# Softmax denominators spread to the heads' rows through DRAM instead of through TensorE

## The chip, the cores and the metric

The kernel runs on one core of one Trainium2 chip. The metric is the time of one execution on the device in microseconds (us), median of several runs. All numbers in this document are of this kernel: run times, one profiled execution, and the answers of its trace. A core has five engines that each follow their own instruction queue in order: TensorE (PE in the profile, with its weight loads as PEld), VectorE (DVE), ScalarE (ACT), GpSimd (POOL) and SyncE (SP). [...] Transfers are issued by SP, ACT or POOL and run on the core's 16 DMA engines.

## The reference

The input x is (2, 256, 64, 64), float32. Layer 0 is attention over all 4096 pixels of an image, with 8 heads of 32 channels, and a 1x1 convolution behind it:

```python
q = proj(Wq, bq) / math.sqrt(hd)
k = proj(Wk, bk)
v = proj(Wv, bv)
attn = jax.nn.softmax(jnp.einsum('bnd,bmd->bnm', q, k), axis=-1)
fuse = jnp.einsum('bnm,bmd->bnd', attn, v)
fuse = fuse.transpose(0, 2, 1).reshape(B, C, H, W)
hybrid = _conv1x1(jnp.concatenate([x, fuse], axis=1), Wf, bf)
return hybrid * m + x * (1.0 - m)
```

Layer 1 is a channel gate, attention in windows of 8x8 pixels with 4 heads, two grouped 7x7 convolutions with normalisation, and a sigmoid gate:

```python
x = x * jax.nn.sigmoid(a.transpose(0, 3, 1, 2))
...
attn = jax.nn.softmax(jnp.einsum('whqd,whkd->whqk', q, k) * hd ** (-0.5), axis=-1)
...
y = lax.conv_general_dilated(x, sa_w1, (1, 1), [(3, 3), (3, 3)], dimension_numbers=dn, feature_group_count=cr)
...
y = lax.conv_general_dilated(y, sa_w2, (1, 1), [(3, 3), (3, 3)], dimension_numbers=dn, feature_group_count=cr)
...
return x * jax.nn.sigmoid(y)
```

What the change touches is the division in layer 0's softmax: fuse is the sum of exp(score) times v, divided by the sum of exp(score), one such sum for each head and each query pixel.

## The kernel before

The program has three parts in time. First (to about 186 us) q, k and v of both images are computed and stored in DRAM. Then comes a long pipeline over 1024 slots (to about 2754 us), and then a tail that finishes the convolutions (to the end at 2980 us).

A slot is one (image b, chunk c of 512 query pixels, head group g of four heads, block m of 128 keys): 2 x 8 x 2 x 32. In a slot, `scores` lets TensorE compute the scores of four heads (L633) two slots ahead, ScalarE takes their exp (L646, three instructions) into a tile e, `products` multiplies them with v into the accumulator av (L665), and VectorE adds e to a running total of 128 keys x 4 heads x 512 pixels (L667). There are eight buffers for e, so VectorE may be up to eight slots late before an exp has to wait for it. A chunk is 64 slots: its two head groups, one after the other.

After a chunk's last slot its work is handed to a small planner. `at(delay, action)` puts an action into a list, due so many slots later, and `run_later` performs the due ones at the end of each slot. DN is 8. The list for a chunk is: `denominators` (DN: 64 pairs of weight load and matmul records on TensorE, L688, which sum the totals over keys; a ScalarE copy to the tile inv, L695), the reciprocal of inv on VectorE (DN+1, L721), the spread of the reciprocals to the rows of their heads in two halves (DN+2 and DN+4, TensorE L704 and ScalarE L711, into the tile rd), the multiplication f = f * rd on VectorE (DN+5, L724), and `stage` (appended at DN+6). inv holds one reciprocal per head and pixel: at partitions 32q to 32q+7, heads 0 to 7 for the q-th quarter of the chunk's pixels. rd holds the same values repeated over the 32 channels of each head: 128 partitions x 2 x 512. For the very first chunk the steps after the reciprocal are `late` by nine slots, the stage by thirteen.

`stage` is a generator that carries a chunk through the 1x1 convolution and the window attention. `run_stages` gives it one step on every fourth slot. Its first step is L739: eight pairs of matmuls, four with x and then four with f, so that the second half needs L724. Then come L747 (ScalarE), L751 and L753 (VectorE). Its last step puts the chunk's result into xo (L971) and POOL stores it in DRAM (L986).

Each engine runs these instructions in the order in which the program makes them, since the section is scheduled by hand. An instruction that waits therefore holds up all that stands behind it on its engine.

The last chunk's actions run after the slots, in a loop that performs nothing but them and single steps of the convolution `conv` (L1052, L1076). There the last stage's steps and the convolution's alternate. The convolution's results go out by L1111 from POOL and SP.

Of the kernel before, what the change touches and what calls it, by code (L numbers as in the profile page):

```python
# [10 lines left out]
F32 = mybir.dt.float32  # L11
# [20 lines left out]
DN = 8  # L32
# [11 lines left out]
HALVES = (slice(0, 64), slice(64, 128))  # L44
# [12 lines left out]
def conv_seq_kernel(ctx: ExitStack, tc: tile.TileContext, a, out):  # L57
    nc = tc.nc
    const = ctx.enter_context(tc.tile_pool(name="const", bufs=1))
    dram = ctx.enter_context(tc.tile_pool(name="dram", bufs=1, space=bass.MemoryType.DRAM))  # L60
# [11 lines left out]
    def psum2(name):  # L72
        return ps["pair"].tile([P, 2, CH], F32, tag="s", name=name)
# [7 lines left out]
    ident = const.tile([P, P], F32, name="ident")  # L81
# [12 lines left out]
    nc.gpsimd.memset(keysum, 0.0)  # L94
    for h in range(HEADS0):
        nc.gpsimd.memset(keysum[:, h, :, h : h + 1], 1.0)
    spread_h = const.tile([P, KC, HG, HD0], F32, name="spread_h")

    for q in range(4):
        nc.gpsimd.tensor_copy(  # L100
            spread_h[32 * q : 32 * q + 32],
            ident[32 * q : 32 * q + 32, 32 * q : 32 * q + HEADS0]
            .rearrange("p (g j) -> p g j", g=KC)
            .unsqueeze(3)
            .to_broadcast([32, KC, HG, HD0]),
        )


    xo = const.tile([P, KC, WS, WP], F32, name="xo")
    nc.gpsimd.memset(xo, 0.0)  # L110
    cbias1 = const.tile([P, NU], F32, name="cbias1")
# [5 lines left out]
        for c in range(NCHUNK)  # L117
    }

    mask_s = dram.tile([B, NCHUNK, CH], F32, name="masks")  # L120


# [250 lines left out]
    with (  # L373
# [8 lines left out]
        for n in ("WqT", "WkT", "WvT"):  # L382
            t = w0.tile([P, KC, C], F32, name=n)
# [4 lines left out]
        for n in ("bq", "bk"):  # L388

            t = w0.tile([P, KC], F32, name=n)  # L390
# [31 lines left out]
        for i, (b, c) in enumerate(chunks):  # L422
# [43 lines left out]
        for i, (b, c) in enumerate(chunks):  # L466
            s = psum2(f"v0_{b}_{c}")
            sv = s.rearrange("p a (t o) -> p (a t) o", t=2)
            for m in range(4):
                for kc in range(KC):  # L470
# [4 lines left out]
                        start=(kc == 0),  # L475
                        stop=(kc == KC - 1),
# [21 lines left out]
            elif i == 2:  # L498
# [3 lines left out]
                for oc in range(KC):  # L502
                    for kc in range(KC):
# [4 lines left out]
                            start=(kc == 0),  # L508
                            stop=(kc == KC - 1),
# [13 lines left out]
    def pipeline(arm, shifted, pools):  # L523
# [23 lines left out]
        stages = deque()  # L547

        def at(delay, action):
            later.append((now[0] + delay, action))  # L550

        def load_piece(n):
            if n * PB >= len(slots):
                return
            b, c, g, m = slots[n * PB]
            p = m // PB
            nm_ = f"{arm}_{b}_{c}_{g}_{p}"
            k = kvp.tile([P, PB * P], F32, tag="k", name=f"k{nm_}")
# [95 lines left out]
        def products(i):  # L654
            b, c, g, m = slots[i]
            if m == 0:
                acc[0] = avp.tile([P, CH], F32, tag="av", name=f"av{arm}_{i}")
                acc[1] = ep.tile([P, HG, CH], F32, tag="sum", name=f"sum{arm}_{i}", bufs=3)
                totals[b, c, g] = acc[1]
            av, total = acc[0], acc[1]  # L660
            e, v = es[i], vts[b, c, g, m // PB]
            start, stop = m == 0, m == NMB - 1
            for j in range(HG):
                r = slice(32 * j, 32 * j + 32)
                nc.tensor.matmul(av[r, :], v[:, m % PB, r], e[:, j, :], start=start, stop=stop)  # L665
            if m > 0:
                nc.vector.tensor_add(total, first[0] if m == 1 else total, e)  # L667
            e = es.pop(i)
            if start:
                first[0] = e  # L670
            if stop:
                if g == 0:
                    fts[b, c] = fp.tile([P, KC, CH], F32, tag="f", name=f"f{arm}_{b}_{c}")
                f = fts[b, c]
                nc.scalar.copy(f[:, g, :], av)  # L675
                if g == 0:
                    return
                both = [totals.pop((b, c, gg)) for gg in range(KC)]
                inv = fp.tile([P, P], F32, tag="inv", name=f"inv{arm}_{i}")
                rd = fp.tile([P, KC, 4, P], F32, tag="rd", name=f"rd{arm}_{i}")  # L680


                def denominators():
                    s = psum2(f"dn{arm}_{i}")
                    for h in range(HEADS0):
                        for q in range(4):
                            r = slice(32 * q, 32 * q + 32)
                            nc.tensor.matmul(  # L688
                                s[r, 0, 0:P],
                                keysum[:, h].rearrange("p i h -> p (i h)"),  # L690
                                both[h // HG][:, h % HG, q * P : (q + 1) * P],
                                start=(h == 0),
                                stop=(h == HEADS0 - 1),
                            )
                    nc.scalar.copy(inv, s[:, 0, 0:P])  # L695


                def spread(hh):
                    t = psum2(f"rd{arm}_{i}_{hh}")
                    for gg in range(KC):  # L700
                        for q in range(2):
                            r = slice(64 * hh + 32 * q, 64 * hh + 32 * q + 32)
                            for o in HALVES:
                                nc.tensor.matmul(  # L704
                                    t[o, q, gg * P : gg * P + P],
                                    spread_h[r, gg].rearrange("p j d -> p (j d)")[:, o],
                                    inv[r, :],
                                    start=True,
                                    stop=True,
                                )  # L710
                    nc.scalar.copy(  # L711
                        rd[:, :, 2 * hh : 2 * hh + 2, :],
                        t[:, :, 0 : KC * P].rearrange("p q (g n) -> p g q n", g=KC),
                    )

                late = EB + 1 if (b, c) == (0, 0) else 0
                at(DN, denominators)  # L720
                at(DN + 1, lambda: nc.vector.reciprocal(inv, inv))  # L721
                at(DN + 2 + late, lambda: spread(0))
                at(DN + 4 + late, lambda: spread(1))
                at(DN + 5 + late, lambda: nc.vector.tensor_mul(f, f, rd.rearrange("p g q n -> p g (q n)")))  # L724

# [427 lines left out]
        def run_later():  # L1153
            for _ in range(len(later)):
                due, action = later.popleft()
                if due <= now[0]:
                    action()
                else:
                    later.append((due, action))
# [17 lines left out]
        for i, (b, c, g, m) in enumerate(slots):  # L1177
            now[0] = i
            if (b, c, g, m) == (B - 1, NCHUNK - 1, 0, 0):
                for _ in banded:  # L1180
                    pass
                conv = convolve()
                next(conv)
            if m % PB == 0:
                load_piece(i // PB + AHEAD)
            if g == KC - 1 and m == 0:
                nxt = (b, c + 1) if c + 1 < NCHUNK else (b + 1, 0)
                if nxt[0] < B:
                    load_q(*nxt)
            rest = scores(i + 2) if i + 2 < len(slots) else None  # L1190
            products(i)
            if rest:
                rest()
            if g == KC - 1 and m == NMB - 1:
                late = EB + 5 if (b, c) == (0, 0) else 0
                at(DN + 6 + late, lambda b=b, c=c: stages.append(stage(b, c)))
            run_later()
            if i % 5 == 1:
                next(banded, None)
            if i % 4 == 0:  # L1200
                run_stages()
# [102 lines left out]
```

## Time and profile before

| What | us |
|---|---|
| Median of 3 runs | 2982.66 (2981.29 to 2983.53) |
| The profiled execution | 2982.11, its span 2980.3 |
| L633 on TensorE (scores), busy | 1167.4 |
| L665 on TensorE (products), busy | 1091.9 |
| L667 on VectorE (adds), busy | 2198.8 and 73.0 (first adds) |
| L646 on ScalarE (exp), busy | 2038.4 |
| Rest of POOL before L986, waiting for L971 | 2523.8 |
| Granted TensorE clock, mean | 0.996 of full speed |

How to read it: the profile is of one execution, so its span is compared with its own time, 2982.11, and that with the median. "Busy" is the time in which an engine has an instruction in work. Matmuls overlap one another, so the sum of their durations is far above their busy time, and a TensorE that is always busy need not be at its peak. Idle time is shown with what ended it; it matters only where it is on the way to the end. In the timeline a line gives start, duration, engine, line, operation, what it writes and reads, the shape, the count merged into the line, and in brackets the idle time before it and what ended that. L704 and L711 are busy in a small part of the time: 512 records of 0.27 us, several at once, and 32 copies of 0.60 us.

POOL is idle for most of the pipeline: between two groups of L986 stores it waits 155 us or so. SP issues the loads of k and v (256 KB each, one of either every fourth slot) and, up to about slot 860, small stores that build the convolution's weights.

### The profile page before, as it was taken

What the parts mean: (1) busy time and instruction counts of PE and PEld (TensorE: products, weight loads), DVE (VectorE), ACT (ScalarE), POOL (GpSimd) and SP (SyncE); (2) the same over time, 40 slices, a digit from 0 to 9 for tenths busy, and PEclk for the clock granted to TensorE, in tenths of its full rate; (3) what the DMA queues carried; (4) which work ended last, traced back from release to release, by engine and by line L of the source; (5) the groups of instructions that cost most, each with busy time, mean ns of one, the idle gap of its engine ahead of it and who ended that gap; (6) DMA issues with size and microseconds to landing.
All of it is one profiled execution on the core that took longest, in us unless ns stands there. A gap on an engine that the chain in (4) does not pass through costs nothing.

```text
span 2980.3 us, 77927 instructions
## 1 busy us (share of the span) xinstructions
PE 2942.5 (99%) x33674; PEld 928.1 (31%) x33674; DVE 2504.0 (84%) x1348; ACT 2474.1 (83%) x4151; POOL 267.1 (9%) x470
## 2 busy tenths in 40 slices
PE   9999999999999999999999999999999999999997
PEld 3551222222222222222222222222222222222775
DVE  4349999899999999999999999999999999999211
ACT  5569879898989898998989898989899898989433
POOL 8110000000000000000000000000000000000366
PEclk9999999999999999999999999999999999999998
DMA  8545322222242323232222223222323232322474
GB/s 247 198 166 171 119 70 52 78 67 70 54 80 63 81 63 69 72 75 70 65 70 67 70 53 74 63 74 62 68 74 73 68 73 68 101 66 86 128 215 103
DMA packets 224018, 267.12 MB, mean 90 GB/s; under 512 B 113384, under 2 KB 130108, under 8 KB 223408
## 3 DMA queue, kind: packets, MB, share of 16 engines
q1 hardware_dynamic: 200880, 231.47, 27.2%
q0 software_dynamic: 18416, 27.87, 4.6%
q8 instruction: 267, 4.37, 0.6%
q10 hardware_dynamic: 4368, 2.70, 0.3%
q14 instruction: 87, 0.71, 0.1%
HBM read 213.49 MB, written 66.13 MB: 94 GB/s over the span
## 4 chain that ended last, share of the span: by engine, by line
PE 87%; DVE 6%; DMA 2%; ACT 2%; POOL 2%; issue 1%; SPq 1%; DVEq 0%; ACTq 0%
PE sa L633 34%; PE ava L665 32%; DVE suma L667 5%; PE qka L810 4%; PE hya L739 4%; PE vwa L896 2%; PE opa L960 2%; PE v L471 2%; PE q L434 2%; POOL out_dram L1111 2%; PE k L434 1%; DMA out_dram<-za 1%; ACT ea L646 1%; PE sca L844 1%; PE rda L704 1%
## 5 line engine op out<-in xcount | busy, mean ns | idle before, releaser
L667 DVE TENSOR_TENSOR suma<-suma,ea 128x2048 f32<-128x2048 f32 x960 | 2198.8, 2290 | 87.9 <-ACT ea L646 1.4
L646 ACT ACTIVATE ea<-sa 128x512 f32<-128x512 f32 (+1 forms) x3072 | 2038.4, 745 | 74.3 <-PE sa L633 35.8
L633 PE MATMUL sa<-qa,ka 32*64 32x512 f32 x16384 | 1167.4, 613 | 1.5 <-ACT vst L479 1.2
L665 PE MATMUL ava<-ea,va 128*32 128x512 f32 x8192 | 1091.9, 605 | 1.3 <-ACT fa L675 0.3
L633 PEld LDWEIGHTS sa<-qa,ka 32*64 32x64 f32 x16384 | 251.4, 129 | 763.2 <-ACT ea L646 696.9
L665 PEld LDWEIGHTS ava<-ea,va 128*32 128x32 f32 x8192 | 161.6, 108 | 835.1 <-issue 806.2
L986 POOL DMA_DIRECT2D xs<-xo x94 | 65.9, 708 | 2524.0 <-DVE xo L971 2523.8
L1111 POOL DMA_DIRECT2D out_dram<-za x210 | 117.8, 569 | 74.3 <-DVE za L1098 51.3
L810 PE MATMUL qka<-ua,qkv_w 128*128 128x512 f32 x256 | 118.4, 605 | 0.0
L667 DVE TENSOR_TENSOR suma<-ea,ea 128x2048 f32<-128x2048 f32 x32 | 73.0, 2283 | 51.3 <-ACT ea L646 51.3
L1098 DVE TENSOR_TENSOR za<-za,xla 128x768 f32<-128x768 f32 (+1 forms) x16 | 21.7, 1359 | 108.2 <-ACT za L1092 60.1
L1076 PE MATMUL c2a<-yca,wa 32*128 32x192 f32 (+1 forms) x1344 | 99.7, 438 | 3.1 <-ACT za L1086 3.1
L453 DVE TENSOR_REDUCE top<-sq 128x512 f32<-128x2048 f32 x16 | 36.6, 2285 | 77.7 <-ACT sq L447 77.7
L1086 ACT ACTIVATE za<-c2a 128x384 f32<-128x384 f32 (+1 forms) x48 | 26.1, 595 | 90.8 <-DMA out_dram<-za 70.7
L747 ACT ACTIVATE ta<-hya,bf 128x512 f32<-128x512 f32 x32 | 20.3, 684 | 95.4 <-PE hya L739 89.2
L1076 PEld LDWEIGHTS c2a<-yca,wa 32*128 32x128 f32 x1344 | 90.9, 315 | 13.7 <-issue 9.6
L865 ACT ACTIVATE ewa<-ewa,mxwa 128x64 f32<-128x64 f32 x256 | 85.2, 346 | 1.5 <-DVE mxwa L856 1.5
L823 ACT ACTIVATE qka<-qka,qkv_b 128x512 f32<-128x512 f32 x64 | 40.5, 683 | 42.1 <-PE qka L810 41.7
L810 PEld LDWEIGHTS qka<-ua,qkv_w 128*128 128x128 f32 x256 | 46.0, 189 | 71.3 <-issue 46.1
L751 DVE TENSOR_TENSOR ta<-ta,mca 128x512 f32<-128x512 f32 x32 | 22.0, 688 | 54.5 <-ACT ta L747 54.5
L434 PE MATMUL q<-x,WqT 128*128 128x512 f32 x128 | 60.6, 617 | 5.1 <-DMA WqT<-in_WqT_dram 5.1
L896 PE MATMUL vwa<-qkv_w,ua 128*128 128x256 f32 x256 | 59.5, 386 | 0.0
(137 smaller groups left out, 1516.0 us busy)
## 6 DMA issues: line engine op xcount, KB each, us to landing
ka<-ks SPq DMA_DIRECT2D x256, 256.0 KB
va<-vs SPq DMA_DIRECT2D x256, 256.0 KB
wa<-ws SPq DMA_DIRECT2D x17, 896.0 KB
ws<-zeros SPq DMA_DIRECT2D x16, 896.0 KB
xs<-xo POOLq DMA_DIRECT2D x78, 140.0 KB, 6.3
xla<-xs SPq DMA_DIRECT2D x24, 420.0 KB
x<-in_x_dram SPq DMA_DIRECT2D x16, 512.0 KB
qs<-qst SPq DMA_DIRECT2D x16, 512.0 KB
```

The source lines that it names most:

```text
L434: nc.tensor.matmul(s[:, g, :], w[:, kc, g * P : (g + 1) * P], rhs, start=(kc == 0), stop=(kc == KC - 1),)
L633: nc.tensor.matmul(heads[j][o], k[r, cols][:, o], q[r, g, :], start=True, stop=not shifted)
L646: nc.scalar.activation(e[:, h, :], tile, AF.Exp, scale=SCALE0)
L665: nc.tensor.matmul(av[r, :], v[:, m % PB, r], e[:, j, :], start=start, stop=stop)
L667: nc.vector.tensor_add(total, first[0] if m == 1 else total, e)
L739: nc.tensor.matmul(s[:, oc, :], wf[:, kc, oc * P : (oc + 1) * P], f[:, kc - KC, :] if half else xw[kc], start=(kc == 0), stop=(kc == 2 * K ...
L810: nc.tensor.matmul(s[:, j, :], wqkv[:, kc, o : o + P], u[:, kc, :], start=(kc == 0), stop=(kc == KC - 1),)
L865: nc.scalar.activation(e[:, n, :], e[:, n, :], AF.Exp, bias=mx[:, n : n + 1], accum_out=rs[:, n : n + 1],)
L896: nc.tensor.matmul(sv[:, t, :], u[:, kc, t * P : (t + 1) * P], wqkv[:, kc, 2 * C : 3 * C], start=(kc == 0), stop=(kc == KC - 1),)
L986: eng.dma_start(x_s[b, n, p + r0 : p + r1].rearrange("r g w -> g r w"), xo[64 * h : 64 * h + 64, oc, r0 - WS * c : r1 - WS * c, :],)
L1076: nc.tensor.matmul(tiles[j // 2][:, j % 2, 0 : n * W], w[r, d], y[r, 0:n, d : d + W], start=(d == 0), stop=(d == KS - 1),)
L1111: engines[stores % len(engines)].dma_start(dst[b, i, r0:r1, UG * u : UG * u + UG, :], z[p + r0 : p + r1, :, nb * m + n, :],)
```

## The change

The reciprocals are no longer spread by matmuls with a 0/1 matrix (`spread_h`, which is gone with the four POOL copies that build it). `store_inv` stores inv into a DRAM tile inv_s, one per chunk, in four transfers of 8 rows x 512 bytes, and the new `spread` loads it back into rd in eight transfers, one per head, each reading one row of 2 KB into 32 partitions. All twelve are issued by POOL and are put into the plan at DN+1, behind the reciprocal. The loads wait for the stores. The multiplication moves from DN+5 to DN+7 and the stage from DN+6 to DN+8; `late` is added to these two alone. On VectorE, the multiplication thus stands behind six adds after the reciprocal instead of four.

```diff
-    spread_h = const.tile([P, KC, HG, HD0], F32, name="spread_h")
-
-    for q in range(4):
-        nc.gpsimd.tensor_copy(
-            spread_h[32 * q : 32 * q + 32],
...
+    inv_s = {
+        (b, c): dram.tile([HEADS0, CH], F32, name=f"invs_{b}_{c}")
+        for b in range(B)
+        for c in range(NCHUNK)
+    }
...
-                def spread(hh):
-                    t = psum2(f"rd{arm}_{i}_{hh}")
-                    for gg in range(KC):
-                        for q in range(2):
-                            r = slice(64 * hh + 32 * q, 64 * hh + 32 * q + 32)
-                            for o in HALVES:
-                                nc.tensor.matmul(
-                                    t[o, q, gg * P : gg * P + P],
-                                    spread_h[r, gg].rearrange("p j d -> p (j d)")[:, o],
-                                    inv[r, :],
-                                    start=True,
-                                    stop=True,
-                                )
-                    nc.scalar.copy(
-                        rd[:, :, 2 * hh : 2 * hh + 2, :],
-                        t[:, :, 0 : KC * P].rearrange("p q (g n) -> p g q n", g=KC),
-                    )
+                def store_inv():
+                    for q in range(4):
+                        nc.gpsimd.dma_start(
+                            inv_s[b, c][:, q * P : (q + 1) * P], inv[32 * q : 32 * q + HEADS0]
+                        )
+
+                def spread(gg):
+                    for h in range(HG):
+                        nc.gpsimd.dma_start(
+                            rd[32 * h : 32 * h + 32, gg].rearrange("p q n -> p (q n)"),
+                            inv_s[b, c][HG * gg + h].partition_broadcast(32),
+                        )
 
                 late = EB + 1 if (b, c) == (0, 0) else 0
                 at(DN, denominators)
                 at(DN + 1, lambda: nc.vector.reciprocal(inv, inv))
-                at(DN + 2 + late, lambda: spread(0))
-                at(DN + 4 + late, lambda: spread(1))
-                at(DN + 5 + late, lambda: nc.vector.tensor_mul(f, f, rd.rearrange("p g q n -> p g (q n)")))
+                at(DN + 1, store_inv)
+                for gg in range(KC):
+                    at(DN + 1, lambda gg=gg: spread(gg))
+                at(DN + 7 + late, lambda: nc.vector.tensor_mul(f, f, rd.rearrange("p g q n -> p g (q n)")))
...
-                at(DN + 6 + late, lambda b=b, c=c: stages.append(stage(b, c)))
+                at(DN + 8 + late, lambda b=b, c=c: stages.append(stage(b, c)))
```

More of the change, by code (lines that the diff above doesn't have):

```diff
@@ L96, in conv_seq_kernel @@
         nc.gpsimd.memset(keysum[:, h, :, h : h + 1], 1.0)
-    spread_h = const.tile([P, KC, HG, HD0], F32, name="spread_h")
-    for q in range(4):
-        nc.gpsimd.tensor_copy(
-            spread_h[32 * q : 32 * q + 32],
[L102 to L105, printed above, removed]
-        )
     xo = const.tile([P, KC, WS, WP], F32, name="xo")
@@ L695, in denominators @@
                     nc.scalar.copy(inv, s[:, 0, 0:P])
-                def spread(hh):
-                    t = psum2(f"rd{arm}_{i}_{hh}")
-                    for gg in range(KC):
-                        for q in range(2):
-                            r = slice(64 * hh + 32 * q, 64 * hh + 32 * q + 32)
-                            for o in HALVES:
-                                nc.tensor.matmul(
-                                    t[o, q, gg * P : gg * P + P],
-                                    spread_h[r, gg].rearrange("p j d -> p (j d)")[:, o],
-                                    inv[r, :],
-                                    start=True,
-                                    stop=True,
-                                )
-                    nc.scalar.copy(
-                        rd[:, :, 2 * hh : 2 * hh + 2, :],
-                        t[:, :, 0 : KC * P].rearrange("p q (g n) -> p g q n", g=KC),
-                    )
+                def store_inv():
[9 more added lines that the diff above has]
+                        )
                 late = EB + 1 if (b, c) == (0, 0) else 0
```

## The prediction, made before the changed kernel had run

> **What bounds the kernel now.** I read the engine totals first, then the chain of waits, then the table of windows and the timeline of one chunk. The page says that TensorE hardly ever rests and that the chain that ended last is TensorE's:
>
> ```profile
> PE 2942.5 (99%) x33674; PEld 928.1 (31%) x33674; DVE 2504.0 (84%) x1348; ACT 2474.1 (83%) x4151; POOL 267.1 (9%) x470
> ...
> PE 87%; DVE 6%; DMA 2%; ACT 2%; POOL 2%; issue 1%; SPq 1%; DVEq 0%; ACTq 0%
> ```
>
> Busy TensorE is not yet a bound, so I look at one whole chunk, from one L739 to the next (window table: length, then busy time of PE, PEld, DVE, ACT, POOL, then clock, DMA share, GB/s):
>
> ```profile
> 855.86:1017.36 161.50, 160.97 (x1897) 42.37 (x1897) 151.31 (x78) 144.78 (x247) 5.77 (x8) 1.00 0.28 70
> ```
>
> VectorE is close behind: 151.3 us, and most of its rest is the 0.1 us between dependent adds (2.29 us long, 2.395 us apart). Whether it binds is seen where it really waits. The timeline around the end of chunk 3 shows both engines:
>
> ```profile
> 836.88 1.06 PE L665 MATMUL ava<-ea,va 128*32 128x512 f32 x8
> ...
> 838.92 1.06 PE L665 MATMUL ava<-ea,va 128*32 128x512 f32 x8
> ...
> 839.37 0.94 DVE L721 RECIPROCAL inva<-inva 128x128 f32<-128x128 f32 x1
> 840.23 9.41 DVE L667 TENSOR_TENSOR suma<-suma,ea 128x2048 f32<-128x2048 f32 x4
> ...
> 840.46 0.56 PE L704 MATMUL rda<-inva,spread_h 32*64 32x128 f32 x12 [0.47 <-DVE inva L721]
> ...
> 841.91 1.06 PE L665 MATMUL ava<-ea,va 128*32 128x512 f32 x8
> ...
> 843.95 1.06 PE L665 MATMUL ava<-ea,va 128*32 128x512 f32 x8
> ...
> 846.63 1.07 PE L665 MATMUL ava<-ea,va 128*32 128x512 f32 x8
> ...
> 849.56 1.22 DVE L724 TENSOR_TENSOR fa<-fa,rda 128x1024 f32<-128x1024 f32 x1
> ...
> 859.32 3.17 PE L739 MATMUL hya<-fa,WfT 128*128 128x512 f32 x7
> ```
>
> Read the starts of L665, one per slot: 2.04 us without a spread (836.88 to 838.92), 2.99 with the first (to 841.91, 0.47 of it waiting for the reciprocal), 2.04 again, 2.68 with the second. Both spreads lie whole on TensorE's path. And VectorE, further on in the same view, catches up with TensorE once a chunk and waits for it:
>
> ```profile
> 863.68 0.69 DVE L751 TENSOR_TENSOR ta<-ta,mca 128x512 f32<-128x512 f32 x1 [3.51 <-ACT ta L747]
> ```
>
> So from L739 to L739 TensorE sets the pace, VectorE has 3.5 us spare at L751, and once a chunk TensorE waits for the reciprocal.
>
> [...] 256 KB stores (vs<-vst) land 2.6 us after their issue starts, 1 KB ones (masks) 3.2. [...] xs<-xo takes POOL 697 to 757 ns each while L667 runs on VectorE.
>
> **The change part by part.** It removes, per chunk, 16 matmuls (32 records), 2 ScalarE copies (0.60 us each) and TensorE's wait for the reciprocal. It adds 4 small stores and 8 broadcast loads on POOL, moves the multiplication L724 two slots later and the stage's due time two ticks later.
>
> *Gain.* I take slot length minus 2.04 at both spreads in chunks 1 to 14, from the same timeline: the first is 0.78 in chunk 1, 1.09 in chunk 2, 1.30 in chunks 8, 12 and 14, and 0.95 in the other nine: 14.3 us. The second is 0.64 in all fourteen: 9.0 us. Together 23.3, or 1.66 a chunk. Chunk 0 I count at nothing: there VectorE is the bound (adds 2.395 us apart, each exp waits for an add to free its e buffer) until the first L739. ScalarE's 1.2 us a chunk gives nothing more: at 144.8 of 161.5 it is not the bound. Can VectorE take over? Its spare 3.5 us at L751 shrink by 1.66, and by up to 0.35 if the multiplication's eight DMA semaphores cost seven extra sequencer waits of 50 ns (those before L721 took 21 to 50 ns). Some 1.5 us remain, so the gain is kept whole.
>
> *Is the new chain hidden?* Call L the time from the end of the reciprocal to the landing of the last load. POOL wakes about 0.3 us after a VectorE result (xo to xs<-xo in the trace). Four stores: the nearest rows are POOL issues of up to 32 rows, 0.50 to 0.59 us (xs<-zero, masks<-mh); I take 0.55, so the last starts at 1.95. It lands as masks<-mh does, 3.2 us later (1.7 to 4.7): 5.15. POOL wakes at 5.45, issues eight loads at 0.6 (bn 0.53, bj 0.66, both partition broadcasts), the last starting at 9.65. A landing of 2.6 to 3.3 us (vs<-vst; the first xs<-xo of a group among the attention's loads) gives L = 12.5. From the bounds of each: 9 to 16. L724 in its new place follows six adds: 6 x 2.395 = 14.3 us after the reciprocal. TensorE needs its product at 859.32, which is 19.0 us after the reciprocal's end (840.31) and will be 17.4 when the spreads are gone; less 1.22 for the multiplication and 0.1 for the wake, L may be 16.1 before TensorE waits. With 12.5 even VectorE doesn't wait; behind a late L724 there would stand two adds and then L751, whose spare time takes 1.5 us. The stage itself stays where it is: run_stages acts on every fourth slot, and ticks DN+6 (slot 77 from the chunk's start) and DN+8 (slot 79) both lead to slot 80; in chunk 0 both lead to slot 92. SP's order is untouched; the 512 KB of loads join its k and v loads on engines that are 25 to 31% busy. On POOL nothing stands behind the loads before xs<-xo of the same chunk, 140 us later.
>
> *The last chunk* has no slots to hide in. In the program's order TensorE now has, after the denominators: L1076, both halves of L739, L1052. The before trace:
>
> ```profile
> 2762.65 0.95 DVE L721 RECIPROCAL inva<-inva 128x128 f32<-128x128 f32 x1 [4.20 <-ACT inva L695]
> ...
> 2765.72 1.31 PE L704 MATMUL rda<-inva,spread_h 32*64 32x128 f32 x32
> ...
> 2770.50 3.60 PE L739 MATMUL hya<-fa,WfT 128*128 128x512 f32 x8
> ```
>
> There L739's second half started 6.9 us after the reciprocal's end. Now it starts at L + 0.35 + 1.22 + 0.06. DMA is nearly idle here (7% of the window 2752 to 2767), so L = 11.5, hence 13.1: 6.2 us later, the removed 1.25 us of L704 already in it. Everything after is TensorE, then POOL's and SP's stores, without a gap in the chain: the shift stays to the end.
>
> *At the start* POOL loses four copies (1.6 us); no wait of TensorE there is put on POOL, so nothing.
>
> Sum: -23.3 + 6.2 = -17.1. The profiled execution took 2982.1 (span 2980.3), 0.55 under the median 2982.66, so the median goes to 2965.5.
>
> **Rivals.**
> - *The chain outlasts its cover (slower).* If each landing among the attention's loads takes what xs<-xo's median shows, 6.3 us, L = 0.3+1.65+6.3+0.3+4.2+6.3 = 19.1. Each of 14 chunks then stalls TensorE at L739 by 3.0 and gains 1.66, and the tail loses 13.8: +19+14 = +33, about 3015. It decides from L = 16.9 on, where 14 x (L-17.76) + L - 5.27 is zero. For it: two landings in series, and startup broadcasts (bj) that took 8.7. Against: xs<-xo moves 140 KB four times in small pieces; its first of four lands in 3.1 to 4.2, and startup was crowded.
> - *VectorE takes over half (no change).* If the wait for eight DMAs or a late L724 eats VectorE's spare time, the chunk gains only about 0.8: 14 x 0.8 = 11.2 less 6.2, 2978. For it: 151.3 of 161.5 busy. Against: the 3.5 us at L751.
> - *The tail costs nothing* if later stores were waiting for DMA anyway: 2959. Against: POOL waits 3.4 us for L1098 at 2822.55, so it has no backlog.
>
> **How the numbers follow.** A measurement tells about 0.2%, 6 us, from no change. Forecast 0.60, the free tail 0.08, VectorE 0.15 (most of it within 0.2%, some on either side), the long chain 0.17. Faster 0.71, same 0.11, slower 0.18. The likeliest case alone, with L from 9 to 16, spans 2962 to 2971. The range, 2956 to 2990, takes in the free tail, the VectorE case and a long chain up to L = 17.5; it leaves out about 0.15.
>
> **What would show it.** Right: L739 to L739 about 159.9 us in the window table; no TensorE wait for DVE in mid-kernel; L724 with no idle time before it, or under 2 us; L751's idle time near 1.5 to 2; in the tail one TensorE wait of about 7 us before the second half of L739. Wrong: L739 waiting for L724 in every chunk (long chain), L751's wait gone and exp waiting for adds (VectorE), or POOL issues well above 0.66 us.

## The result, and the profile after

The changed kernel takes 2971.56 us, median of six runs (2969.27 to 2973.90); the kernel before, run beside it, 2982.86 (2981.29 to 2983.53). The ratio is 0.996, 95% interval [0.995, 0.9971]: faster, by some 11 us. The profiled execution took 2969.57, its span is 2967.5, so its distance from before's span is 12.8 us.

In what follows, "shift" is the start of an instruction in a kernel's span less the start of the same instruction in the span of before. It is read from the two traces and says where time came or went. For the changed kernel it is -25.0 us at the last denominators (L681), -18.7 after the last chunk's 1x1 convolution (L725), -12.4 at the fourteenth of the tail's sixteen gating products (L1084), and -12.8 at the end. So the pipeline gained what was hoped for, and half of it was given back in two places. A shift is read from one execution: at the last denominators it is -22.2 to -24.1 in the eight further kernels below whose loop works like that of the change, so one such figure is good to 2 or 3 us.

The page of the changed kernel, busy time by engine and the shares of the chain that ended last:

```profile
PE 2927.6 (99%) x33162; PEld 915.5 (31%) x33162; DVE 2502.4 (84%) x1348; ACT 2459.3 (83%) x4119; POOL 361.9 (12%) x658
...
PE 92%; DVE 3%; POOL 2%; DMA 1%; ACT 1%; issue 1%; SPq 0%; DVEq 0%; ACTq 0%; POOLq 0%
```

TensorE is still the bound, with 512 records and 15 us less. One whole chunk, from one first half of the 1x1 convolution to the next (window table; columns as in the prediction):

```profile
849.31:1009.24 159.93, 159.86 (x1866) 41.51 (x1865) 150.97 (x78) 143.81 (x245) 11.73 (x20) 1.00 0.30 74
```

161.50 has become 159.93. What the instructions that use the reciprocals waited for, in the whole kernel, is told by the view of the multiplication's line, L710:

```profile
its engine sat idle before it (us, times) until:
  DMA rda<-invs: 10.2, 1
who waited for it (us, times):
  PEld hya L725: 6.8, 2
  PE hya L725: 5.6, 1
```

One wait in sixteen chunks: in fifteen of them the loads landed before VectorE came to the multiplication. The one is in the tail. Its timeline:

```profile
2737.62 0.95 DVE L706 RECIPROCAL inva<-inva 128x128 f32<-128x128 f32 x1 [4.18 <-ACT inva L688]
2738.86 2.01 POOL L693 DMA_DIRECT2D invs<-inva  x4 [136.46 <-DVE inva L706]
2740.70 3.70 PE L725 MATMUL hya<-xa,WfT 128*128 128x512 f32 x8
2742.62 3.95 POOL L699 DMA_DIRECT2D rda<-invs  x8 [1.75 <-DMA invs<-inva]
2748.73 1.23 DVE L710 TENSOR_TENSOR fa<-fa,rda 128x1024 f32<-128x1024 f32 x1 [10.16 <-DMA rda<-invs]
2750.01 5.43 PE L725 MATMUL hya<-fa,WfT 128*128 128x512 f32 x8 [5.61 <-DVE fa L710]
```

TensorE waits 5.61 us, and then the second half takes 5.43 us for the same eight matmuls that took 3.60 before. The window table of the same stretch says why (the column after the five engines' busy times is the granted TensorE clock):

```profile
2742.50:2746.70 4.20, 1.90 (x5) 0.57 (x3) 0.00 (x0) 0.04 (x1) 3.95 (x8) 1.00 0.31 94
2746.70:2750.10 3.40, 0.09 (x1) 0.09 (x1) 1.37 (x2) 0.00 (x0) 0.00 (x0) 0.50 0.11 39
2750.10:2753.50 3.40, 3.40 (x4) 1.41 (x5) 1.06 (x2) 0.00 (x0) 2.65 (x4) 0.50 0.37 62
```

The idle time has cost TensorE its clock: 0.50 for 6.8 us, 3.4 of them while it works again. In e3_warm below, where further matmuls leave only 2.00 us of the wait, the clock stays at 1.00 and the eight matmuls take 3.70. Other half-speed stretches of this study lasted 3.4 us (before, after its first chunk) and 10.2 (e8_merge, with a wait of 7.98).

The second place is in the tail's convolutions. Four lines of the timeline after:

```profile
2829.03 8.31 POOL L1097 DMA_DIRECT2D out_dram<-za  x15 [1.69 <-issue]
...
2832.37 0.39 SPq L1017 DMA_DIRECT2D xla<-xs  x1
...
2839.42 0.87 ACT L1072 ACTIVATE za<-c2a 128x384 f32<-128x384 f32 x2 [10.40 <-DMA out_dram<-za]
2839.96 4.87 PE L1062 MATMUL c2a<-yca,wa 32*128 32x192 f32 x52 [5.73 <-ACT za L1072]
```

and the same four of before:

```profile
2849.45 5.11 POOL L1111 DMA_DIRECT2D out_dram<-za  x9 [0.34 <-issue]
...
2850.93 0.39 SPq L1031 DMA_DIRECT2D xla<-xs  x1
...
2852.85 0.87 ACT L1086 ACTIVATE za<-c2a 128x384 f32<-128x384 f32 x2 [5.25 <-DMA out_dram<-za]
2853.39 3.56 PE L1076 MATMUL c2a<-yca,wa 32*128 32x192 f32 x52 [0.56 <-ACT za L1086]
```

Read them from below. TensorE waits for ScalarE, ScalarE for the stores of an earlier result, which hold one of the two buffers of z. The last of these stores is the 72nd that GpSimd issues, one of those merged into the first line. The view of this one store, after and before (the middle line says who waited for it):

```profile
L1097 POOL DMA_DIRECT2D out_dram<-za x1: 582/582/582, 2833.4 to 2833.4; - x1
...
DMA to landing us min/median/max: 5.6/5.6/5.6
```

```profile
L1111 POOL DMA_DIRECT2D out_dram<-za x1: 584/584/584, 2850.6 to 2850.6; - x1
...
  ACT za L1086: 5.3, 1
...
DMA to landing us min/median/max: 1.8/1.8/1.8
```

In the change it is issued at 2833.39, 1.02 us behind SP's load of the next rows (420 KB, with 896 KB of weights right after it); it lands at 2839.03, and ScalarE goes on 0.4 us later. In before it is issued at 2850.61, 0.32 us ahead of that load, and lands after 1.8. Up to the 63rd store GpSimd and the convolutions had kept step in both: the gating product at 2828.74 (2847.32 in before) starts 24.8 us after the 25th store. But GpSimd, which here issues one store after another without rest, then paused 1.69 us ahead of its 64th store ("issue": it waited for nothing that the profile shows). In before the pause of this kind was 0.34, ahead of the 70th, and no pause in the run was over 0.43. The wait of TensorE went from 0.56 to 5.73 us and again halved its clock, from 2838.9 to 2845.7.

### The profile page after: what moved, and what is told of

Its sections match the earlier page's. It is cut to its first block, busy times and chain, and to the rows that moved or that the text cites. A ratio compares the mean times of both kernels' runs of the same rounds, so it can differ in the third digit from the quotient of the medians.

```text
span 2967.5 us, 77160 instructions
## 1 busy us (share of the span) xinstructions
PE 2927.6 (99%) x33162; PEld 915.5 (31%) x33162; DVE 2502.4 (84%) x1348; ACT 2459.3 (83%) x4119; POOL 361.9 (12%) x658
## 4 chain that ended last, share of the span: by engine, by line
PE 92%; DVE 3%; POOL 2%; DMA 1%; ACT 1%; issue 1%; SPq 0%; DVEq 0%; ACTq 0%; POOLq 0%
PE sa L626 35%; PE ava L658 33%; PE qka L796 4%; PE hya L725 4%; PE q L427 2%; PE vwa L882 2%; DVE suma L660 2%; PE k L427 2%; PE opa L946 2%; PE v L464 2%; POOL out_dram L1097 2%; PE c2a L1062 1%; PE dna L681 1%; DMA out_dram<-za 1%; PE c1a L1038 1%
## 5 line engine op out<-in xcount | busy, mean ns | idle before, releaser
L1084 DVE TENSOR_TENSOR za<-za,xla 128x768 f32<-128x768 f32 (+1 forms) x16 | 21.7, 1359 | 115.6 <-ACT za L1078 75.8
L693 POOL DMA_DIRECT2D invs<-inva x64 | 32.7, 518 | 659.2 <-DVE inva L706 486.3
L1062 PEld LDWEIGHTS c2a<-yca,wa 32*128 32x128 f32 x1344 | 92.0, 315 | 19.4 <-issue 9.6
L699 POOL DMA_DIRECT2D rda<-invs x128 | 63.3, 502 | 30.5 <-DMA invs<-inva 30.5
```

The lines of the kernel that those rows point to most:

```text
L699: nc.gpsimd.dma_start(rd[32 * h : 32 * h + 32, gg].rearrange("p q n -> p (q n)"), inv_s[b, c][HG * gg + h].partition_broadcast(32),)
L1062: nc.tensor.matmul(tiles[j // 2][:, j % 2, 0 : n * W], w[r, d], y[r, 0:n, d : d + W], start=(d == 0), stop=(d == KS - 1),)
```

## The experiments

The table has what the traces of all kernels say. "Pause" is GpSimd's longest pause between two output stores in its unbroken run of them in the convolutions (for e8_merge: just behind that run), with the number of stores issued before it. The next four columns are of the stretch from the end of the last chunk's 1x1 convolution to the fourteenth gating product. "72nd store" is how long before SP's load of rows, the one behind the first gating product, GpSimd issues that store (minus: behind it); "z wait" is TensorE's idle time before the second convolution's matmuls; "half clock" is the time at half speed; "lost there" is the change of the shift. "Lost at L739" is that across the last chunk's 1x1 convolution. Ratios are to before, run on the same chip beside each kernel. All columns behind the ratio are of one profiled execution, which in these kernels took from 4.2 us less to 2.9 us more than the median.

| Kernel | Median us | Ratio [95%] | Lost at L739 | Pause us (store) | 72nd store | z wait | Half clock | Lost there |
|---|---|---|---|---|---|---|---|---|
| before | 2982.86 | | | 0.43 (37) | 0.3 | 0.6 | 0 | |
| after | 2971.56 | 0.9960 [0.9950, 0.9971] | 6.4 | 1.69 (63) | -1.0 | 5.7 | 6.8 | 6.2 |
| e1_hybrid | 2961.72 | 0.9923 [0.9909, 0.9937] | 0 | 1.18 (68) | -0.3 | 3.5 | 3.4 | 3.9 |
| e2_last_only | 2991.34 | 1.0021 [1.0014, 1.0028] | 6.8 | 1.51 (64) | 1.3 | 1.2 | 3.4 | 5.5 |
| e3_warm | 2968.96 | 0.9947 [0.9932, 0.9962] | 4.4 | 1.32 (63) | -0.7 | 4.7 | 6.8 | 5.1 |
| e4_dn5 | 2975.47 | 0.9970 [0.9961, 0.9979] | 7.0 | 1.59 (63) | -1.0 | 5.3 | 6.8 | 5.9 |
| e5_after60 | 2969.73 | 0.9953 [0.9938, 0.9968] | 7.0 | 2.24 (45) | 1.0 | 0.6 | 0 | 2.4 |
| e6_hybrid60 | 2960.66 | 0.9924 [0.9911, 0.9938] | 0 | 2.21 (48) | 1.2 | 2.4 | 3.4 | 4.4 |
| e7_hops | 2993.77 | 1.0034 [1.0021, 1.0047] | 5.9 | 1.99 (62) | -0.7 | 5.5 | 6.8 | 7.0 |
| e8_merge | 2971.58 | 0.9957 [0.9942, 0.9972] | 9.8 | 2.01 (89) | 0.6 | 0.3 | 0 | 1.4 |
| e9_after156 | 2972.92 | 0.9966 [0.9953, 0.9980] | 6.9 | 1.66 (63) | -0.8 | 4.8 | 6.8 | 6.9 |
| e10_hybrid156 | 2964.99 | 0.9936 [0.9922, 0.9950] | 0 | 1.77 (68) | -1.2 | 5.7 | 6.8 | 6.0 |
| e11_after24 | 2974.82 | 0.9971 [0.9960, 0.9982] | 6.2 | 1.84 (63) | -1.2 | 6.0 | 6.8 | 7.1 |
| e12_hybrid24 | 2962.77 | 0.9929 [0.9915, 0.9942] | 0 | 1.63 (68) | -0.7 | 4.9 | 3.4 | 5.8 |

**The change in all chunks but the last, and in the last alone.** Both keep `spread_h` and the old spread as `spread_mm`; e2_last_only has `!=` where e1_hybrid has `==`:

```diff
+                mm = (b, c) == (B - 1, NCHUNK - 1)
+                if mm:
+                    at(DN + 2 + late, lambda: spread_mm(0))
+                    at(DN + 4 + late, lambda: spread_mm(1))
+                else:
+                    at(DN + 1, store_inv)
...
-                at(DN + 7 + late, lambda: nc.vector.tensor_mul(f, f, rd.rearrange("p g q n -> p g (q n)")))
+                at((DN + 5 if mm else DN + 7) + late, lambda: nc.vector.tensor_mul(f, f, rd.rearrange("p g q n -> p g (q n)")))
```

> The last chunk's reciprocals are spread by the old matmuls, all others through DRAM. Theory A (all that the change loses, it loses by the last chunk's chain): the tail runs as before the change, so the time is that of before less the 25.0 us gained up to the last denominators: 2957.9, between 2956 and 2960, with L739's second half at 3.6 us and no half-clock stretch before the very end. Rival R (the later wait of 5 us in the convolutions comes from the 180 further transfers on POOL in the pipeline, not from the last chunk): 2963 to 2967, with a long wait of L1072's counterpart for the output stores again.

> Only the last chunk goes through DRAM, all others by matmul. Theory A: before plus what the tail loses, 6.4 us at L739 and 0 to 6.3 in the convolutions: 2989 to 2996. Rival R (the convolutions' share comes from the pipeline's transfers): 2989 and no more. If the tail cost nothing, 2983.

e1_hybrid is the fastest version of the study, with e6_hybrid60 below (0.9924): 0.9923 against 0.996 for the change as it is, with intervals that don't meet. Its timeline in the tail:

```profile
2739.49 0.95 DVE L735 RECIPROCAL inva<-inva 128x128 f32<-128x128 f32 x1 [4.18 <-ACT inva L699]
2745.41 1.23 DVE L744 TENSOR_TENSOR fa<-fa,rda 128x1024 f32<-128x1024 f32 x1 [4.97 <-ACT rda L728]
2747.35 3.60 PE L759 MATMUL hya<-fa,WfT 128*128 128x512 f32 x8
```

With matmuls the multiplication starts 4.97 us after the reciprocal, not 10.16, and TensorE waits for nothing. Yet its convolutions still lost 3.9 us, so its time lies between what theory A and rival R had. e2_last_only is slower than before by 0.21%, within theory A's span: without the chunks' gain the last chunk's chain is a loss. It lost 5.5 us in the convolutions without any of the loop's transfers. So neither theory explains both losses. It shows one thing more. Its first fifteen chunks are those of before, yet its shift at the last denominators is -2.1, and it is there from the first chunk on. The window tables of before and after for the time after the first chunk's 1x1 convolution explain it. Before:

```profile
411.00:414.00 3.00, 3.00 (x24) 0.20 (x8) 2.97 (x2) 1.69 (x3) 0.00 (x0) 0.50 0.93 231
```

After:

```profile
411.00:414.00 3.00, 3.00 (x44) 0.55 (x32) 2.96 (x2) 2.43 (x5) 0.00 (x0) 1.00 0.80 237
```

In the profiled execution of before, two short waits of TensorE (0.98 and 0.68 us) were followed by 3.4 us at half speed, 1.6 us lost. In the change, with the same two waits (0.97 and 0.68 us), it didn't come, nor in e1_hybrid, e2_last_only and e4_dn5 (1.00 in the same windows). 1.6 us of every shift here are thus no merit of the change.

**TensorE kept warm in the tail.** The first half of the last chunk's L725 is computed twice, which changes nothing in its result:

```diff
-            for half in range(2):
+            again = (b, c) == (B - 1, NCHUNK - 1)
+            for n, half in enumerate((0, 0, 1) if again else (0, 1)):
...
-                            stop=(kc == 2 * KC - 1),
+                            stop=(kc == 2 * KC - 1 or (again and n == 0 and kc == KC - 1)),
```

> The changed kernel, with the first half of the last chunk's L739 done twice (3.5 us of TensorE work in its wait of 5.6 us; the result is the same). Theory A (TensorE's idle time halved its clock, and that cost 1.8 us at L739's second half on top of the wait): second half 3.6 us instead of 5.4, everything to the first convolution's end 1.8 us earlier, median about 2969.7 or lower. Rival (the clock fell for another reason): second half 5.4 us again and 2971.6.

The timeline of that stretch, of e3_warm:

```profile
2742.47 7.13 PE L726 MATMUL hya<-xa,WfT 128*128 128x512 f32 x16
2751.60 3.70 PE L726 MATMUL hya<-fa,WfT 128*128 128x512 f32 x8 [2.00 <-DVE fa L710]
```

3.4 us of useless matmuls filled most of the wait, the second half is back at 3.70 us, and the loss there fell from 6.4 to 4.4 us. So 4.4 is the chain's own price, and the rest is the clock's. The run times are too close to tell the two kernels apart (0.9947 [0.9932, 0.9962] against 0.996).

**The multiplication back in its old slot:**

```diff
-                at(DN + 7 + late, lambda: nc.vector.tensor_mul(f, f, rd.rearrange("p g q n -> p g (q n)")))
+                at(DN + 5 + late, lambda: nc.vector.tensor_mul(f, f, rd.rearrange("p g q n -> p g (q n)")))
...
-                at(DN + 8 + late, lambda b=b, c=c: stages.append(stage(b, c)))
+                at(DN + 6 + late, lambda b=b, c=c: stages.append(stage(b, c)))
```

> The changed kernel with the multiplication back at DN+5 and the stage at DN+6: four adds stand between reciprocal and multiplication, 9.3 us, where the loads land 10.5 to 13.5 us after the reciprocal. Theory A (VectorE has spare time at the stage's first multiplication, and TensorE needs the product only 17.4 us after the reciprocal): VectorE waits 1 to 4 us at L710 in each chunk, TensorE doesn't, the chunk stays at 159.9 and the time at 2971.6 within 3. Rival (VectorE takes over as the bound): a chunk is longer by 1 us or more, 2985 or above.

The view of the multiplication's line in e4_dn5:

```profile
its engine sat idle before it (us, times) until:
  DMA rda<-invs: 38.2, 12
```

One of the twelve waits is the tail's, of 10.0 us; VectorE waits 2.6 us on average in the eleven others, and in none of those chunks does TensorE wait for the multiplication. The time is not told apart from the change's (0.997 [0.9961, 0.9979]). VectorE had that much to spare, and the later slot is not what the gain rests on.

**A longer chain.** Two more DRAM copies on the way, in every chunk but the last:

```diff
+                def hop(n):
+                    src = hop_s[(b, c), n - 1] if n else inv_s[b, c]
+                    nc.gpsimd.dma_start(hop_s[(b, c), n], src)
...
                 at(DN + 1, store_inv)
+                for n in range(hops):
+                    at(DN + 1, lambda n=n: hop(n))
```

> The changed kernel, in which the reciprocals go through two more DRAM memories on their way in every chunk but the last (two more transfers one after the other, 16 KB each, of 0.5 us issue and some 3 us landing). Theory A (16.1 us of TensorE's other work cover the chain): the chain grows from about 11 to 13 us to about 18 to 20, TensorE then waits for the multiplication about 2 to 4 us in each of the 15 chunks, the period of a chunk grows from 159.9 to 162 to 164 us, and the median goes to about 3000 to 3030. Rival (the cover is longer than I reckoned, or VectorE's other work ends the wait anyway): the period stays at 159.9, the time at 2971 to 2975.

The rows of the second half of L740 (L725 of the change) in two chunks of e7_hops:

```profile
856.66 5.40 PE L740 MATMUL hya<-fa,WfT 128*128 128x512 f32 x8 [2.01 <-DVE fa L725]
...
1828.16 3.70 PE L740 MATMUL hya<-fa,WfT 128*128 128x512 f32 x8 [3.00 <-DVE fa L725]
```

From the third chunk on the multiplication started 16.1 to 19.4 us after the reciprocal's end. In the chunk whose multiplication started 16.1 us after it TensorE waited for nothing; at 16.3 it waited 0.2, at 16.9 0.6, at 18.2 and later 2.0 to 3.1. The cover is the 16.1 us of the prediction, and the rival falls. All waits together make 14.9 us in eleven chunks. My 3000 to 3030 was too high because the landings were shorter than I took them, not because of the cover. The price of a wait isn't its length, though: that of 2.01 us and one of 2.22 made their chunks 4.0 and 4.2 us longer, those of 3.00 and 3.13 only 3.3 and 3.4, with the clock whole. The clock in windows just after one of either kind:

```profile
1342.00:1345.00 3.00, 3.00 (x5) 1.22 (x4) 2.90 (x2) 0.00 (x0) 0.00 (x0) 0.50 0.00 0
...
1828.00:1831.00 3.00, 2.84 (x7) 1.41 (x8) 2.90 (x3) 0.00 (x0) 0.00 (x0) 1.00 0.00 0
```

**Fewer, larger loads.** One load for each group of four heads:

```diff
-                    for h in range(HG):
-                        nc.gpsimd.dma_start(
-                            rd[32 * h : 32 * h + 32, gg].rearrange("p q n -> p (q n)"),
-                            inv_s[b, c][HG * gg + h].partition_broadcast(32),
-                        )
+                    nc.gpsimd.dma_start(
+                        rd[:, gg].rearrange("p q n -> p (q n)"),
+                        inv_s[b, c][HG * gg : HG * gg + HG].unsqueeze(1).to_broadcast([HG, 32, CH]),
+                    )
```

> The changed kernel with each group's four loads made one (2 loads a chunk instead of 8, the same bytes). Theory A (the issue of 8 loads by GpSimd, 0.50 us each, is 3 to 4 us of the chain): the chain is about 3 us shorter, in the tail TensorE's wait for the last multiplication falls from about 4.5 to about 1.5 to 3 us; with the clock's half speed gone or not, the median goes to 2966 to 2970. In the middle of the kernel nothing changes (period 159.9). Rival (the landing grows with the size of a load, so that the last row arrives at the same time): the wait in the tail stays at 4.5 us, the time at 2971.

The tail of e8_merge:

```profile
2749.66 1.42 POOL L698 DMA_DIRECT2D rda<-invs  x2 [2.83 <-issue]
...
2757.01 1.22 DVE L709 TENSOR_TENSOR fa<-fa,rda 128x1024 f32<-128x1024 f32 x1 [12.53 <-DMA rda<-invs]
2758.29 6.48 PE L724 MATMUL hya<-fa,WfT 128*128 128x512 f32 x8 [7.98 <-DVE fa L709]
```

My theory fell, and the rival understated it. Issue went from 3.95 us for eight loads to 1.42 for two, but the multiplication waits 12.53 us instead of 10.16: 2.83 of it is a pause of POOL ahead of the loads, and the last landing comes 7.2 us after the loads' start instead of 5.8. In the other chunks the last landing came 11.8 to 14.8 us after the reciprocal, with eight loads 10.2 to 14.1. The landing is what counts. Why the larger loads land later isn't shown: the edit changes their shape too (the outer step counts four heads instead of 32 rows), and no run tells that from their size. In the convolutions, on the other hand, this kernel lost only 1.4 us; its time isn't told apart from the change's (0.9957 against 0.996).

**Where GpSimd pauses.** Four kernels have additional small stores of the reciprocals into DRAM that nobody reads, at a time when GpSimd is idle. That of 60:

```diff
+    more_s = [dram.tile([HEADS0, CH], F32, name=f"mores_{n}") for n in range(15)]
...
+                def store_more():
+                    for t in more_s:
+                        for q in range(4):
+                            nc.gpsimd.dma_start(
+                                t[:, q * P : (q + 1) * P], inv[32 * q : 32 * q + HEADS0]
+                            )
...
+                if (b, c) == (1, 0):
+                    at(DN + 3, store_more)
```

> The changed kernel with 60 more small stores of the reciprocals into DRAM memory that nobody reads, issued by GpSimd in the middle of the kernel (batch 1's first chunk), where it is idle; nothing else differs. Theory A (the second loss of 4 to 6 us, in the last convolutions, comes of a pause of GpSimd's transfer queue of 1.3 to 2.7 us whose place depends on how many transfers went before): the pause moves away from the 65th output store, the convolutions lose less than 2 us against before, and the median goes from 2971.6 to about 2966 (ratio 0.9945). Theory B (the loss comes of the earlier arrival of the convolutions or of the clock alone, not of the number of transfers): the shift still falls by 4 to 6 us there, the time stays at 2971 (0.996).

> The kernel with the last chunk's reciprocals spread by matmuls and all others through DRAM, with the same 60 more small stores in batch 1's first chunk. Theory A (place of the pause): the 3.9 us that this kernel lost in its last convolutions come back in large part, the median goes from 2961.7 to about 2958 to 2959 (ratio 0.9915). Theory B: as without them, 2961.7 (0.9923).

GpSimd's rows with the pause, of e5_after60:

```profile
2821.49 18.43 POOL L1107 DMA_DIRECT2D out_dram<-za  x33 [2.24 <-issue]
```

and of e11_after24, where it stayed in the place that it has in the change:

```profile
2831.71 8.32 POOL L1107 DMA_DIRECT2D out_dram<-za  x15 [1.84 <-issue]
```

With 60 stores the pause came 18 to 20 stores earlier. In e5_after60 TensorE's wait for z fell from 5.7 to 0.6 us, its clock stayed whole, and 2.4 us were lost instead of 6.2, nearly as theory A has it. In e6_hybrid60 the wait fell too, from 3.5 to 2.4, but 4.4 us were lost, not fewer than without: a wait of 2.39 us was left, now ahead of the first gating product, and cost the clock again. Neither kernel's time is told apart from that of the kernel without the 60 stores (0.9953 against 0.996, 0.9924 against 0.9923). So neither theory holds as it stood. I took it then that a pause anywhere in GpSimd's unbroken run hurts, and tried to put it outside, with 156 stores and with 24:

```diff
-    more_s = [dram.tile([HEADS0, CH], F32, name=f"mores_{n}") for n in range(15)]
+    more_s = [dram.tile([HEADS0, CH], F32, name=f"mores_{n}") for n in range(13)]
...
-                if (b, c) == (1, 0):
+                if b == 1 and c < 3:
```

(for 24 only the first of these lines differs from that of 60, with range(6)).

> The changed kernel with 156 more small stores that nobody reads, 52 in each of batch 1's first three chunks, where GpSimd is idle. 60 of them moved GpSimd's pause from the 63rd output store to the 45th, which is still inside the stretch (25th to 78th) that GpSimd alone stores without a rest; 156 should move it by some 47 stores, to about the 16th, ahead of that stretch, and the next to about the 137th, behind it. Theory A' (the pause costs only inside that stretch): the convolutions then lose less than 1.5 us (6.2 with none, 2.5 with 60 more), the median goes to about 2965 to 2967. Theory B (the loss has nothing to do with the place of the pause): it stays at 3 to 6 us, the time at 2969 to 2972.

> The kernel with the last chunk's reciprocals spread by matmuls and all others through DRAM, with 156 more small stores that nobody reads, 52 in each of batch 1's first three chunks. With 60 of them the pause stood at the 48th output store, inside the stretch that GpSimd alone stores without a rest, and the convolutions lost 4.4 us. Theory A' (the pause costs only inside that stretch): it moves to about the 16th store, the convolutions lose less than 1.5 us, and the ratio goes from 0.9923 to about 0.991. Theory B: as before, 0.9923.

> The changed kernel with 24 more small stores that nobody reads in batch 1's first chunk. 156 of them had left GpSimd's pause at the 63rd output store, as without any, and 60 had moved it to the 45th: both fit a place that comes round every 52 of them, that is every 121 output stores. 24 should then move it by 24 / 52 x 121 = 56 stores, to about the 7th, ahead of the stretch (25th to 78th) that GpSimd alone stores without a rest, and the next to about the 128th, behind it. Theory A' (the pause costs only inside that stretch): the shift against before falls by less than 1.5 us in the convolutions (6.2 without them), the ratio goes to about 0.9945. Theory B: it falls by 3 to 7 us as in the other runs, the ratio stays at 0.996.

> The kernel with the last chunk's reciprocals spread by matmuls and all others through DRAM, with 24 more small stores in batch 1's first chunk. The pause should move from the 68th output store to about the 12th and the 133rd. Theory A': the convolutions lose less than 1.5 us (3.9 without them, 6.0 with 156), the ratio goes to about 0.991. Theory B: they lose 4 to 6 us, the ratio stays at 0.992 to 0.994.

All four failed as tests: neither 156 stores (52 in each of three chunks) nor 24 moved the pause, which stayed at stores 63 and 68 (e12_hybrid24 had another, of 1.42, at the 47th), with 5.8 to 7.1 us lost. The rule by which I placed it is wrong. What the fourteen traces show together is this: the order of two transfers goes with the long wait, not the pause alone. In nine kernels GpSimd's 72nd store goes out 0.3 to 1.2 us behind SP's load of rows, and TensorE's next wait for z is 3.0 to 6.0 us long. In the other five, before among them, it goes out 0.3 to 1.3 us ahead of the load, and that wait is 0.7 us or less. A pause matters so far as it turns this order: e2_last_only has one of 1.51 us ahead of its 65th store, and still sends the 72nd in time. That the late store makes ScalarE and so TensorE wait is read from the timeline; no run moves the load alone, so the order as the cause is not tested by an edit. The order isn't the whole loss either: e2_last_only, e5_after60, e6_hybrid60 and e8_merge lost 1.4 to 5.5 us with the store in time, in shorter waits for z elsewhere, in waits of 1.4 to 2.2 us for the rows themselves (not in e5_after60), and in two of them by the clock. What sets the place of the pause stays open, and so does how much of the loss would go with a pause put outside the run in the hybrid.

## Why the prediction was right or wrong

- **Range and sign.** 2971.56 lies in 2956 to 2990 and on the faster side. It is 6 us above the 2965.5 named, just above the likeliest case's own span of 2962 to 2971.
- **Gain of the chunks, -23.3: right.** The shift at the last denominators is -25.0, and 1.6 of it is before's half-speed stretch after the first chunk; 23.4 are left. In the eight other kernels it is 20.6 to 22.5, so the close match is in part luck. The period is 159.93 (predicted 159.9), and the first chunk, taken at nothing, gave nothing.
- **The chain hidden in mid-kernel: right,** with a sum made of wrong terms. The last landing came 9.8 to 14.1 us after the reciprocal's end, 11.0 in the middle of sixteen chunks (I had 12.5, from 9 to 16). The loads took 0.50 us to issue (I had 0.6), and the last of the stores mostly landed 1.5 us after the start of its issue (I had 3.2). The cover of 16.1 was measured in e7_hops. From issue to landing the stores took 1.6 us and the loads 3.1, both medians. The margin is smaller than this trace alone shows: in the other kernels with the same chain the last landing came up to 15.8 us after the reciprocal (e5_after60).
- **VectorE keeps pace: right.** Its wait of 3.51 us at L751 (L737 of the change) is 1.35 to 1.93 from the third chunk to the fifteenth, as predicted. In e4_dn5 it could even wait 2.6 us a chunk more without holding TensorE up.
- **The last chunk, +6.2: right in size, wrong in its parts.** The shift lost 6.4, of which the chain is about 4.4 (L was 9.8 in the tail, not 11.5) and TensorE's halved clock 2. I had no term for the clock. That the two errors cancel is luck.
- **"Everything after is TensorE, then POOL's and SP's stores, without a gap in the chain: the shift stays to the end": wrong.** This is the step that failed. 6.2 us of the shift were lost in the convolutions, where TensorE's supply hangs on two buffers of z and GpSimd's stores have no rest: TensorE waited 5.73 us for z, behind a store that went out after SP's loads, and its clock fell again. What I leaned on ("it has no backlog") was one wait of POOL at 2822.55; behind it, from about the 25th store on, GpSimd was one unbroken row of issues. The sum by the traces: -23.4 - 1.6 + 6.4 + 6.2 = -12.4, as at the fourteenth gating product; at the end it is -12.8. The range held only since it was wide enough for a loss that it had no term for.
- **Rivals.** The long chain decides from L = 16.9 in my sum; the largest L was 14.1 (15.8 in the other kernels). VectorE's and the free tail's cases fell.

## What to carry to other kernels

A spread by transfers pays where other work covers its whole chain (here some 11 us, with 16.1 of cover, in fifteen chunks) and costs where nothing does; use both forms, one in the loop and the other in the last round. Price a wait of TensorE by its clock too: in e7_hops a wait of 2.01 us made its chunk 4.0 us longer, with the clock at 0.50 behind it, and one of 3.00 us only 3.3, with the clock at 1.00. And follow a gain to the end of the kernel through every stage with two buffers and a busy store queue, since an earlier start doesn't carry through them on its own: here one store that went out 1 us behind a large load, and no longer 0.3 us ahead of it, came with 5 us more of waiting.

## What the runs showed of the hardware that wasn't expected

- The granted clock fell after waits of quite different length. In the tail of the change waits of 5.61 and 5.73 us of TensorE were each followed by half speed, from 2746.71 to 2753.54 and from 2838.87 to 2845.70. In before two waits of 0.98 and 0.68 us were enough for 3.4 us of it; the change's two of 0.97 and 0.68 in the same place were not.
- Nor did the longer wait always cost more. In e7_hops the clock was 0.50 for 3.4 us behind the wait of 2.01 us, and 1.00 behind that of 3.00. In the 3.41 us before the clock fell, at 857.30, TensorE was busy for 41%; in the two stretches of that length around the wait of 3.00 us, for 55% and 57% (TensorE's busy time is the second number after the window):

```profile
853.89:857.30 3.41, 1.40 (x4) 0.40 (x3) 1.92 (x2) 0.00 (x0) 0.00 (x0) 1.00 0.09 30
...
1823.27:1826.69 3.42, 1.88 (x5) 0.57 (x3) 0.00 (x0) 0.00 (x0) 0.00 (x0) 1.00 0.24 13
1826.69:1830.10 3.41, 1.94 (x5) 0.99 (x6) 3.23 (x2) 0.00 (x0) 0.00 (x0) 1.00 0.00 0
```

- What made the clock fall behind one wait and not behind the other is not shown: no run changes where a wait lies and nothing else. Busy shares rest on modelled ends of matmuls, so they are rough.
- GpSimd paused in its row of output stores where the profile shows nothing that it waited for: in the change 1.69 us behind the 63rd store and 2.67 behind the 184th, in before 0.34 behind the 69th and 2.21 behind the 190th, 121 stores apart in both. In e8_merge a pause of 2.83 fell ahead of the last chunk's two loads.
- In e8_merge two loads of four heads each landed later than eight of one head in the change, with the same bytes: in the tail 7.2 us after the first one's start, against 5.8.
